# Layer 1 of a convolution-attention hybrid: turning 128x128 squares by DVE and DMA, or by PE

## The chip, the cores and the metric

The kernel runs on one core of a Trainium2 chip. The metric is the device time of one execution in microseconds (us). A core has a matrix engine (TensorE, PE in the profile; its weight loads are listed as PEld), a vector engine (VectorE, DVE), an activation engine (ScalarE, ACT), GpSimd (POOL), and SyncE (SP), which here only issues DMA transfers. Each engine works through a queue of its own, in the order in which the program was laid out for it, and semaphores hold an instruction until what it needs is there. Matrix products go to PSUM, everything else lives in SBUF.

## What is computed

The input x has 4 images of 128 channels and 64x64 pixels, all float32. Two layers follow each other, for each image b:

```python
# layer 0: attention over 4096 pixels, 64 inner channels
q, k, v = wq @ x, wk @ x, wv @ x                 # [64, 4096]
x = x + wo @ (softmax(k.T @ q) @ v.T).T
# layer 1, on tokens t = x.T  [4096, 128]
h = layernorm(t)
t = t + softmax(causal((h @ Wq) @ (h @ Wk).T / sqrt(128))) @ (h @ Wv)
h = layernorm(t)
u = batchnorm(h @ W.T)                           # statistics over all 4 * 4096 tokens
y[n] = sigmoid(u[n] + y[n - 1] @ V.T)            # a scan over the tokens
out = t + y
```

## The kernel before

The whole work sits in `fast_path`. (A second function, `general_path`, runs behind a flag if some number left its safe range; it does not run here.) `xs` keeps all four images in SBUF.

**Blocks and items.** A block is 512 query columns of one image and one layer: 8 blocks of layer 0 and then 8 blocks of layer 1 for each image, 64 in all, 32 of them in layer 1. A block's keys are taken in tiles of 128, two tiles to an item. A layer-0 block has 16 items. A layer-1 block g is causal: it has 2g full items and two partial ones (896 and 384 columns), so the first has 2 items and the last 16. Full layer-1 items take PE about 3.44 us, layer-0 items about 1.72 us.

**One step of the main loop** (L767 to L793) writes down, in this order: the scores of item s (L638: PE products into `s_ps`, then ACT's exponential into `p`, and in layer 1 POOL's causal mask of the diagonal squares); the values of item s - 2 (L699: PE accumulates `acc`); if that item was its block's last, also the copy of `acc` to `agg` (ACT), the sum `den` of the two halves of the denominators (DVE, L733), the row products of a coming block (`r_ps`, L512) and a transposition that was put off; then the sums of item s (L679: DVE adds `p` to `dsum`); and last one task that is due.

**The tasks behind a block.** A generator names each next task with a number of steps. For layer 1 (`finish1`, L583) it is:

- `first`, 1 step after the block's last values: `project` (L517) and `normed` (L536). `project` makes the denominators: `den` holds, for 128 key lanes and 512 queries, sums that must still be added over the 128 lanes, with the result by query on partitions. Four PE transposes put `den` into PSUM (`den_ps`, L521), and one DVE reduce of 128x512 (L523) adds along the free axis. Then a reciprocal (L524), four products with the value weights (`o_ps`, L527) and four DVE updates of the tokens in `xs` (L532). `normed` is the layer norm by tokens, on DVE with one POOL operation: statistics (L541, L542), variance (L544), a power on POOL (L429), three to four tiny DVE operations (L430 to L433), four scalings (L548). Its result is the tile `xh2` (in the profile `xh`).
- `second`, 3 steps later: the tokens before the norm are turned to channels by four PE transposes (`tT_ps`), copied by ACT and stored to DRAM (L596); the normed tokens are turned by four PE transposes as well (`xh2T_ps`, L556) and copied by DVE into `xhT2` (L557).
- `third`, 1 step later: the product with W (`wx_ps`, L602), its batch statistics by DVE (L605) and a copy by ACT into `xs` (L607).

One task runs in a step, the one that has been due longest; where none is due, a piece of the next image's layer-0 keys (`cols0`, `vals0`, `vals0_by_tokens`) is done instead. `finish0` does the same as `first` for layer 0.

**Who sets the order.** The program text gives each engine a sequence, but the framework's scheduler lays the queues out by its own estimate of when an instruction's inputs and buffers are there, so that in the timeline neighbours of the text can be parted, or an instruction can stand ahead of others that precede it in the text. The PSUM tiles of all side work (`den_ps`, `o_ps`, `r_ps`, `tT_ps`, `xh2T_ps`, `wx_ps`, `kr_ps`, ...) share one tag with two banks (`misc`, L443). The pool `work` gives each of its tags two buffers. All transfers in the main loop (`swap<-kr` L475, `xs<-in_xT` L505, `x<-xc` L596) go through SP's queue in order.

**The end.** After the last block, the batch norm's scale is made, and the scan runs in 28 steps of chunks (L825), with the residual and the stores behind it.

Of the kernel before, what the change touches and what calls it, by code (L numbers as in the profile page):

```python
# [9 lines left out]
F32 = mybir.dt.float32  # L10
AF = mybir.ActivationFunctionType
ALU = mybir.AluOpType
AX = mybir.AxisListType
PSUM = bass.MemoryType.PSUM

P = 128
BLK = 512
# [325 lines left out]
def fast_path(  # L343
# [21 lines left out]
    nc = tc.nc  # L365
    B, C, N = x.shape
    M = c_wqT.shape[1]
    assert C == P and M == P // 2 and N % CHUNK == 0
    NT = N // P
    NB = N // BLK  # L370
    TPB = BLK // P
# [2 lines left out]
    WARM, TOL, STEPS = 12, 1e-6, 16  # L374
    NCH = N // STEPS
    CPB = BLK // STEPS

    const = ctx.enter_context(tc.tile_pool(name="const", bufs=1))
    xpool = ctx.enter_context(tc.tile_pool(name="x", bufs=1))
# [32 lines left out]
    ident = const.tile([P, P], F32, name="ident")  # L412
# [6 lines left out]
    nc.gpsimd.memset(mhalf, -0.5)  # L419
    minus = const.tile([P, P], F32, name="minus")  # L420
    nc.vector.tensor_scalar(minus, ident, -1.0, None, ALU.mult)
    good = const.tile([P, 1], F32, name="good")
    g1 = const.tile([P, P], F32, name="g1")
    recs = const.tile([P, 2, B, NT], F32, name="recs")
# [10 lines left out]
    with tc.tile_pool(name="batch", bufs=1) as batch, tc.tile_pool(name="rows", bufs=2) as rowp, tc.tile_pool(  # L435
        name="prob", bufs=4
    ) as prob, tc.tile_pool(name="work", bufs=2) as wk, tc.tile_pool(name="stat", bufs=4) as stat, tc.tile_pool(
        name="ps_s", bufs=2, space=PSUM
    ) as ps_s, tc.tile_pool(name="ps_a", bufs=1, space=PSUM) as ps_a, tc.tile_pool(
        name="ps_m", bufs=2, space=PSUM  # L440
    ) as ps_m:

        def misc(name):  # L443
            return ps_m.tile([P, BLK], F32, tag="m", name=name)
# [72 lines left out]
        def project(layer, b, g, agg, den):  # L517

            dp = misc("den_ps")
            for j in range(TPB):  # L520
                nc.tensor.transpose(dp[:, ts(j, P)], den[:, ts(j, P)], ident)  # L521
            rec = recs[:, layer, b, ts(g, TPB)]
            nc.vector.tensor_reduce(rec, dp.rearrange("p (j k) -> p j k", k=P), AX.X, ALU.add)  # L523
            nc.vector.reciprocal(rec, rec)  # L524
            op = misc("o_ps")
            for j in range(TPB):
                nc.tensor.matmul(  # L527
                    op[:, ts(j, P)], lhsT=agg[:, ts(j, P)], rhs=wv1 if layer else wo2, start=True, stop=True
                )
            for j in range(TPB):  # L530
                t = xs[:, b, ds(g * BLK + j * P, P)]
                nc.vector.scalar_tensor_tensor(  # L532
                    t, in0=op[:, ts(j, P)], scalar=rec[:, j : j + 1], in1=t, op0=ALU.mult, op1=ALU.add
                )

        def normed(b, g, dst):  # L536

            st = stat.tile([P, TPB, nc.vector.BN_STATS_DIM], F32, tag="st", name="ln_st")
            mv = stat.tile([P, TPB, nc.vector.BN_AGGR_DIM], F32, tag="mv", name="ln_mv")
            for j in range(TPB):  # L540
                nc.vector.bn_stats(st[:, j], xs[:, b, ds(g * BLK + j * P, P)])  # L541
                nc.vector.bn_aggr(mv[:, j], st[:, j])  # L542
            var = stat.tile([P, TPB], F32, tag="var", name="ln_var")
            nc.vector.tensor_scalar(var, mv[:, :, 1], LN_EPS, None, ALU.add)  # L544
            y = stat.tile([P, TPB], F32, tag="rstd", name="ln_rstd")
            rsqrt(y, var, stat.tile([P, TPB], F32, tag="z", name="ln_z"))
            for j in range(TPB):
                nc.vector.tensor_scalar(  # L548
                    dst[:, j], xs[:, b, ds(g * BLK + j * P, P)], mv[:, j, 0:1], y[:, j : j + 1], ALU.subtract, ALU.mult
                )  # L550

        def transposed(src, dst, name, engine):

            ps = misc(name)
            for j in range(TPB):
                nc.tensor.transpose(ps[:, ts(j, P)], src[:, j], ident)  # L556
            engine(dst, ps)  # L557

        def in_range():

            r = recs.rearrange("p l b t -> p (l b t)")
            r2 = stat.tile([P, 2 * B * NT], F32, tag="r2", name="r2")
            nc.vector.tensor_scalar(r2, r, LOW, None, ALU.is_ge)
            nc.vector.tensor_scalar(r, r, HIGH, None, ALU.is_le)
            nc.vector.tensor_tensor(r, r, r2, ALU.mult)
            nc.vector.tensor_reduce(good, r, AX.X, ALU.add)

        def finish0(b, g):

            agg, den = bs[b].agg, bs[b].den  # L570

            def norm():
                if g == 0:
                    bs[b].xh = batch.tile([P, NT, P], F32, tag="xh", name="xh")
                    bs[b].xhT = batch.tile([P, N], F32, tag="xhT", name="xhT")
                normed(b, g, bs[b].xh[:, ts(g, TPB)])

            yield 2, lambda: (project(0, b, g, agg, den), norm())
            fill.append(
                lambda: transposed(bs[b].xh[:, ts(g, TPB)], bs[b].xhT[:, ts(g, BLK)], "xhT_ps", nc.scalar.copy)  # L580
            )

        def finish1(b, g):  # L583
            agg, den = bs[b].agg, bs[b].den
            mem = {}

            def first():
                project(1, b, g, agg, den)
                mem["xh"] = wk.tile([P, TPB, P], F32, tag="xh2", name="xh2")
                normed(b, g, mem["xh"])  # L590

            def second():
                t = xs[:, b, ts(g, BLK)].rearrange("p (j c) -> p j c", c=P)
                xc = wk.tile([P, BLK], F32, tag="xc", name="xc")
                transposed(t, xc, "tT_ps", nc.scalar.copy)
                nc.sync.dma_start(out=x2[b, :, ts(g, BLK)], in_=xc)  # L596
                mem["xhT"] = wk.tile([P, BLK], F32, tag="xhT2", name="xhT2")
                transposed(mem["xh"], mem["xhT"], "xh2T_ps", nc.vector.tensor_copy)

            def third():  # L600
                wp = misc("wx_ps")
                nc.tensor.matmul(wp, lhsT=wf, rhs=mem["xhT"], start=True, stop=True)  # L602
                if b == B - 1 and g == NB - 1:
                    in_range()
                nc.vector.bn_stats(stats[:, b * NB + g], wp)  # L605

                nc.scalar.copy(  # L607
                    xs[:, b, ts(g, BLK)].rearrange("p (s c) -> p s c", c=CPB),
                    wp.rearrange("p (c s) -> p s c", s=STEPS),
                )  # L610

            yield 1, first
            yield 3, second
            yield 1, third


        class Item:
# [183 lines left out]
    with tc.tile_pool(name="xr", bufs=1) as xrp, tc.tile_pool(name="y", bufs=2) as yp, tc.tile_pool(  # L801
        name="ps_y", bufs=2, space=PSUM
# [15 lines left out]

        by_step = xs.rearrange("p b (g s c) -> p b s g c", s=STEPS, c=CPB)
        start = xrp.tile([P, B, NCH + 1], F32, name="start")  # L820
        nc.gpsimd.memset(start[:, :, 0:1], 0.0)
        prev = [None] * B
        grid = lambda t: t.rearrange("p (g c) -> p g c", c=CPB)

# [23 lines left out]
        def residual(b):  # L848

            for h in range(2):  # L850
                for g in range(h * NB // 2, (h + 1) * NB // 2):
                    y = yp.tile([P, BLK], F32, tag="yt", name="yt")
                    nc.scalar.copy(  # L853
                        y.rearrange("p (c s) -> p c s", s=STEPS),
                        xs[:, b, ts(g, BLK)].rearrange("p (s c) -> p c s", c=CPB),
                    )
# [10 lines left out]
        for b in range(B):  # L867
# [3 lines left out]
            sq = yp.tile([P, NCH], F32, tag=f"y{b}", name="sq")  # L871
# [69 lines left out]
```

## Time and profile before

| | |
|---|---|
| median of 7 runs | 2188.41 us (2187.5 to 2191.7) |
| the profiled execution | 2190.2 us, its span 2188.4 us |
| PE busy | 2113.9 us, 97% of the span, mean granted clock 0.988 |
| DVE busy | 1440.4 us, 66% |
| ACT busy | 1057.2 us, 48% |
| POOL busy | 104.5 us, 5% |
| 4 x L521 `den_ps`, 64 blocks of both layers | 256 records, 280 ns each by the record |
| 4 x L556 `xh2T_ps`, 32 blocks | 128 records, 285 ns each by the record |
| L523 reduce of `den_ps` (DVE) | 64 records, 684 ns each |
| L557 copy of `xh2T_ps` (DVE) | 32 records, 691 ns each |
| L602 `wx_ps` | 64 records (two for each product) |
| L596 `x<-xc`, issue on SP / to landing | 0.32 us / 2.0 us |
| L475 `swap<-kr`, issue on SP / to landing | 0.47 us / 2.2 us |
| L505 `xs<-in_xT`, issue on SP / to landing | 0.46 us / 3.1 us |

In span order there is a start of some 34 us (loads and the first keys), then for each image about 238 us of layer 0 and 275 us of layer 1, and from 2075 us on the tail with the scan. PE runs matrix instructions pipelined, so the lengths of its records overlap: what a group really occupies is read from the starts of the groups before and behind it, or from the chain of waits. An f32 product is two records, an f32 transpose one. "Idle before" is the time in which an engine stood still before an instruction, with the instruction that ended the wait.

### The profile page before, as it was taken

What the parts mean: (1) busy time and instruction counts of PE and PEld (TensorE: products, weight loads), DVE (VectorE), ACT (ScalarE), POOL (GpSimd) and SP (SyncE); (2) the same over time, 40 slices, a digit from 0 to 9 for tenths busy, and PEclk for the clock granted to TensorE, in tenths of its full rate; (3) what the DMA queues carried; (4) which work ended last, traced back from release to release, by engine and by line L of the source; (5) the groups of instructions that cost most, each with busy time, mean ns of one, the idle gap of its engine ahead of it and who ended that gap; (6) DMA issues with size and microseconds to landing.
All of it is one profiled execution on the core that took longest, in us unless ns stands there. A gap on an engine that the chain in (4) does not pass through costs nothing.

```text
span 2188.4 us, 30521 instructions
## 1 busy us (share of the span) xinstructions
PE 2113.9 (97%) x12204; PEld 940.7 (43%) x12204; DVE 1440.4 (66%) x2703; ACT 1057.2 (48%) x1162; POOL 104.5 (5%) x207
## 2 busy tenths in 40 slices
PE   6999999999999999999999999999999999999973
PEld 2333354444333345444333335444433334544452
DVE  2888865444788875544588886445488887544486
ACT  3666633333566643333466653333356664333278
POOL 0000010000000010000000001000000001000000
PEclk9999999999999999999999999999999999999986
DMA  6000011000000001000000001100000000000033
GB/s 222 1 1 1 1 30 49 5 5 5 6 1 1 1 15 44 20 10 5 6 1 1 1 1 39 39 5 6 5 6 1 1 1 6 10 10 5 6 159 155
DMA packets 30134, 48.74 MB, mean 22 GB/s; under 512 B 3104, under 2 KB 20256, under 8 KB 28448
## 3 DMA queue, kind: packets, MB, share of 16 engines
q1 hardware_dynamic: 28096, 46.15, 6.1%
q8 instruction: 98, 1.61, 0.3%
q10 hardware_dynamic: 1888, 0.56, 0.1%
q14 instruction: 52, 0.43, 0.1%
HBM read 25.72 MB, written 16.78 MB: 19 GB/s over the span
## 4 chain that ended last, share of the span: by engine, by line
PE 91%; ACT 4%; DVE 2%; DMA 1%; POOL 0%; issue 0%; SPq 0%; ACTq 0%; DVEq 0%
PE s_ps L658 21%; PE acc L717 21%; PE s_ps L649 20%; PE acc L709 19%; PE o_ps L527 2%; ACT yt L853 1%; PE den_ps L521 1%; PE wx_ps L602 1%; ACT xs L841 1%; PE r_ps L512 1%; PE kr_ps L469 1%; ACT y L841 1%; PE xhT_ps L556 1%; DVE dsum L689 1%; PE xh2T_ps L556 1%; PE v_ps L481 1%
## 5 line engine op out<-in xcount | busy, mean ns | idle before, releaser
L689 DVE TENSOR_TENSOR dsum<-dsum,p 128x1024 f32<-128x1024 f32 x676 | 828.0, 1225 | 466.0 <-ACT p L665 336.7
L663 ACT ACTIVATE p<-s_ps,nshift 128x1024 f32<-128x1024 f32 x512 | 571.4, 1116 | 357.5 <-PE s_ps L649 338.0
L665 ACT ACTIVATE p<-s_ps 128x1024 f32<-128x1024 f32 (+2 forms) x288 | 274.2, 952 | 564.0 <-PE s_ps L658 462.5
L709 PE MATMUL acc<-p,v 64*64 64x512 f32 x4096 | 532.5, 590 | 1.7 <-ACT half L728 1.7
L649 PE MATMUL s_ps<-swap,kr 64*64 64x512 f32 x2048 | 530.0, 595 | 1.9 <-DMA swap<-kr 1.9
L649 PE MATMUL s_ps<-kr 64*64 64x512 f32 x2048 | 530.0, 595 | 0.0
L658 PE MATMUL s_ps<-rows,xhT 128*128 128x512 f32 (+3 forms) x1152 | 504.0, 559 | 0.0
L717 PE MATMUL acc<-p,xh 128*128 128x512 f32 (+3 forms) x1152 | 501.6, 558 | 0.0
L717 PEld LDWEIGHTS acc<-p,xh 128*128 128x128 f32 x1152 | 216.1, 191 | 240.8 <-issue 231.4
L658 PEld LDWEIGHTS s_ps<-rows,xhT 128*128 128x128 f32 x1152 | 211.4, 190 | 226.7 <-issue 189.4
L709 PEld LDWEIGHTS acc<-p,v 64*64 64x64 f32 x4096 | 155.6, 133 | 284.5 <-issue 265.5
L649 PEld LDWEIGHTS s_ps<-swap,kr 64*64 64x64 f32 x2048 | 137.6, 133 | 133.1 <-issue 123.9
L649 PEld LDWEIGHTS s_ps<-kr 64*64 64x64 f32 x2048 | 137.6, 133 | 128.2 <-issue 123.6
L429 POOL TENSOR_TENSOR ln_rstd<-ln_var,mhalf 128x4 f32<-128x4 f32 x64 | 66.1, 1033 | 1221.3 <-DVE ln_var L544 1221.3
L697 DVE TENSOR_TENSOR dsum<-dsum,p 128x256 f32<-128x256 f32 (+1 forms) x120 | 55.9, 499 | 72.4 <-POOL p L669 72.4
L687 DVE COPY dsum<-p 128x1024 f32<-128x1024 f32 x60 | 41.4, 690 | 69.7 <-ACT p L665 57.6
L532 DVE SCALAR_TENSOR_TENSOR xs<-o_ps,recs,xs 128x128 f32<-128x128 f32 x256 | 73.0, 344 | 8.9 <-PE o_ps L527 2.8
L548 DVE TENSOR_SCALAR xh<-xs,ln_mv,ln_rstd 128x128 f32<-128x128 f32 x256 | 71.3, 342 | 2.2
L669 POOL TENSOR_SCALAR_AFFINE_SELECT p<-p 128x128 f32<-128x128 f32 x128 | 34.4, 292 | 681.8 <-ACT p L665 681.8
L541 DVE BATCH_NORM_STATS2 ln_st<-xs 128x6 f32<-128x128 f32 x256 | 63.5, 270 | 0.0
L607 ACT COPY xs<-wx_ps 128x512 f32<-128x512 f32 x32 | 18.7, 584 | 69.5 <-DVE stats L605 69.5
L840 DVE SCALAR_TENSOR_TENSOR z<-xs,scale,y_ps 128x256 f32<-128x256 f32 x108 | 48.5, 480 | 4.9 <-DMA xr<-x 3.4
(101 smaller groups left out, 1106.6 us busy)
## 6 DMA issues: line engine op xcount, KB each, us to landing
xs<-in_x SPq DMA_DIRECT2D x16, 512.0 KB, 8.4
xs<-in_xT SPq DMA_DIRECT2D x32, 256.0 KB, 3.1
x<-xc SPq DMA_DIRECT2D x32, 256.0 KB, 2.0
xr<-x SPq DMA_DIRECT2D x4, 2048.0 KB, 12.0
out_x<-xr SPq DMA_DIRECT2D x8, 1024.0 KB, 3.9
swap<-kr SPq DMA_DIRECT2D x32, 128.0 KB, 2.2
wo<-in_c_woT ACTq DMA_DIRECT2D x2, 32.0 KB, 4.3
wqT<-in_a_wqT ACTq DMA_DIRECT2D x1, 64.0 KB, 5.5
```

The lines of the kernel that those rows point to most:

```text
L429: nc.gpsimd.tensor_tensor(y, var, mhalf[:, : y.shape[-1]], ALU.pow)
L532: nc.vector.scalar_tensor_tensor(t, in0=op[:, ts(j, P)], scalar=rec[:, j : j + 1], in1=t, op0=ALU.mult, op1=ALU.add)
L541: nc.vector.bn_stats(st[:, j], xs[:, b, ds(g * BLK + j * P, P)])
L548: nc.vector.tensor_scalar(dst[:, j], xs[:, b, ds(g * BLK + j * P, P)], mv[:, j, 0:1], y[:, j : j + 1], ALU.subtract, ALU.mult)
L649: nc.tensor.matmul(ps[c * M : c * M + M, off : off + n], lhsT=bs[it.b].kr[part, h, ds(t % (NT // 2) * P + c * M, M)], rhs=rows[h], start=True,
L658: nc.tensor.matmul(ps[:, off : off + n], lhsT=lhsT, rhs=rhs, start=True, stop=True)
L663: nc.scalar.activation(it.p[:, :off], ps[:, :off], AF.Exp, bias=nshift)
L665: nc.scalar.activation(it.p[:, :off], ps[:, :off], AF.Exp, scale=float(P) ** -0.5)
L689: nc.vector.tensor_tensor(flat, flat, it.p, ALU.add)
L697: nc.vector.tensor_tensor(den[:, h, q0:], den[:, h, q0:], it.p[:, o : o + n], ALU.add)
L709: nc.tensor.matmul(bt.acc[h * M : h * M + M, r], lhsT=bt.v[part, t], rhs=it.p[part, o : o + n], start=it.first, stop=it.last,)
L717: nc.tensor.matmul(bt.acc[:, 0, q0:], lhsT=bt.xh[:, t], rhs=it.p[:, o : o + n], start=it.first and h == 0, stop=it.last and h == 1,)
```

## The change

It touches layer 1 alone, and of it two places; layer 0 keeps its PE transposes.

- **Denominators** (`project`, all 32 layer-1 blocks). In place of four PE transposes and a DVE reduce, DVE turns `den` in squares of 32x32 (`sq`), and one DVE reduce adds each square's rows: `part`, 128 partitions by 16 columns. One PE product with a constant matrix `fold` (the identity folded to add the four 32-partition groups and repeat the sum on each) gives 16 columns, of which each partition needs four: DVE multiplies by the mask `quarter` (`own`) and reduces to the four columns of `rec`.
- **Normed tokens** (`finish1`, 31 of the 32 blocks; the last keeps the old way). In place of four PE transposes and a DVE copy, DVE turns the tokens in 32x32 squares into `sqT`, and 16 transfers on SP's queue, each of 32 partitions by four runs of 128 bytes, place the squares in `xhT2`. For these blocks `third` comes 4 steps after `second` instead of 1.
- Two constants, `fold` and `quarter`, are built by eight DVE operations at the start. A scratch tile of the range test moves into the tag `den`.

```diff
--- before.py
+++ after.py
@@ -374,6 +374,8 @@
     WARM, TOL, STEPS = 12, 1e-6, 16
     NCH = N // STEPS
     CPB = BLK // STEPS
+    S = nc.vector.STREAM_SQUARE_SIZE
+    Q = P // S
 
     const = ctx.enter_context(tc.tile_pool(name="const", bufs=1))
     xpool = ctx.enter_context(tc.tile_pool(name="x", bufs=1))
@@ -419,6 +421,17 @@
     nc.gpsimd.memset(mhalf, -0.5)
     minus = const.tile([P, P], F32, name="minus")
     nc.vector.tensor_scalar(minus, ident, -1.0, None, ALU.mult)
+    fold = const.tile([P, P], F32, name="fold")
+    nc.vector.tensor_reduce(
+        fold[:, :S], ident.rearrange("p (q r) -> p r q", r=S), AX.X, ALU.add
+    )
+    for q in range(1, Q):
+        nc.vector.tensor_copy(fold[:, ts(q, S)], fold[:, :S])
+    quarter = const.tile([P, TPB, Q], F32, name="quarter")
+    for j in range(TPB):
+        nc.vector.tensor_reduce(quarter[:, j], ident.rearrange("p (q r) -> p q r", r=S), AX.X, ALU.add)
     good = const.tile([P, 1], F32, name="good")
     g1 = const.tile([P, P], F32, name="g1")
     recs = const.tile([P, 2, B, NT], F32, name="recs")
@@ -517,10 +530,24 @@
         def project(layer, b, g, agg, den):
 
             dp = misc("den_ps")
-            for j in range(TPB):
-                nc.tensor.transpose(dp[:, ts(j, P)], den[:, ts(j, P)], ident)
             rec = recs[:, layer, b, ts(g, TPB)]
-            nc.vector.tensor_reduce(rec, dp.rearrange("p (j k) -> p j k", k=P), AX.X, ALU.add)
+            if layer:
+                sq = wk.tile([P, TPB * Q, S], F32, tag="sq", name="sq")
+                nc.vector.transpose(out=sq.rearrange("p a b -> p (a b)"), in_=den)
+                part = stat.tile([P, TPB * Q], F32, tag="part", name="part")
+                nc.vector.tensor_reduce(part, sq, AX.X, ALU.add)
+                nc.tensor.matmul(dp[:, : TPB * Q], lhsT=fold, rhs=part, start=True, stop=True)
+                own = stat.tile([P, TPB, Q], F32, tag="own", name="own")
+                nc.vector.tensor_tensor(
+                    own, dp[:, : TPB * Q].rearrange("p (j q) -> p j q", q=Q), quarter, ALU.mult
+                )
+                nc.vector.tensor_reduce(rec, own, AX.X, ALU.add)
+            else:
+                for j in range(TPB):
+                    nc.tensor.transpose(dp[:, ts(j, P)], den[:, ts(j, P)], ident)
+                nc.vector.tensor_reduce(rec, dp.rearrange("p (j k) -> p j k", k=P), AX.X, ALU.add)
             nc.vector.reciprocal(rec, rec)
             op = misc("o_ps")
             for j in range(TPB):
@@ -559,7 +586,7 @@
         def in_range():
 
             r = recs.rearrange("p l b t -> p (l b t)")
-            r2 = stat.tile([P, 2 * B * NT], F32, tag="r2", name="r2")
+            r2 = wk.tile([P, BLK], F32, tag="den", name="r2")[:, : 2 * B * NT]
             nc.vector.tensor_scalar(r2, r, LOW, None, ALU.is_ge)
             nc.vector.tensor_scalar(r, r, HIGH, None, ALU.is_le)
             nc.vector.tensor_tensor(r, r, r2, ALU.mult)
@@ -583,6 +610,7 @@
         def finish1(b, g):
             agg, den = bs[b].agg, bs[b].den
             mem = {}
+            final = b == B - 1 and g == NB - 1
 
             def first():
                 project(1, b, g, agg, den)
@@ -595,7 +623,18 @@
                 transposed(t, xc, "tT_ps", nc.scalar.copy)
                 nc.sync.dma_start(out=x2[b, :, ts(g, BLK)], in_=xc)
                 mem["xhT"] = wk.tile([P, BLK], F32, tag="xhT2", name="xhT2")
-                transposed(mem["xh"], mem["xhT"], "xh2T_ps", nc.vector.tensor_copy)
+                if final:
+                    transposed(mem["xh"], mem["xhT"], "xh2T_ps", nc.vector.tensor_copy)
+                    return
+                sq = wk.tile([P, Q, TPB, S], F32, tag="sqT", name="sqT")
+                nc.vector.transpose(
+                    out=sq.rearrange("p c j t -> p j c t"), in_=mem["xh"].rearrange("p j (c r) -> p j c r", r=S)
+                )
+                to = mem["xhT"].rearrange("p (j q t) -> p j q t", q=Q, t=S)
+                for c in range(Q):
+                    for q in range(Q):
+                        nc.sync.dma_start(out=to[ts(c, S), :, q], in_=sq[ts(q, S), c])
 
             def third():
                 wp = misc("wx_ps")
@@ -611,7 +650,7 @@
 
             yield 1, first
             yield 3, second
-            yield 1, third
+            yield 1 if final else 4, third
 
 
         class Item:
```

## The prediction

> **What bounds the kernel now.** I read the shares and the chain first, then the busy time by stretches, then the timeline at the places the change touches. The page says which engine carries the end:
>
> ```profile
> PE 2113.9 (97%) x12204; PEld 940.7 (43%) x12204; DVE 1440.4 (66%) x2703; ACT 1057.2 (48%) x1162; POOL 104.5 (5%) x207
> PE 91%; ACT 4%; DVE 2%; DMA 1%; POOL 0%; issue 0%; SPq 0%; ACTq 0%; DVEq 0%
> ```
>
> 91% of the chain that ended last is TensorE (PE) work. By stretches (columns: stretch, its length, busy us and instructions of PE, weight load, DVE, ACT, POOL, then PE clock and DMA), the dense first blocks of layer 1, a passage from layer 1 to the next batch's layer 0, a layer-0 part and a layer-1 part:
>
> ```profile
> 270.00:300.00 30.00, 30.00 (x128) 15.08 (x121) 20.33 (x62) 10.86 (x15) 4.56 (x10) 1.00 0.11 27
> 545.00:560.00 15.00, 13.82 (x112) 5.68 (x104) 10.92 (x29) 7.71 (x8) 1.01 (x1) 1.00 0.05 18
> 560.00:790.00 230.00, 228.92 (x2061) 86.48 (x2062) 189.54 (x301) 145.54 (x137) 7.84 (x9) 1.00 0.01 1
> 820.00:1060.00 240.00, 240.00 (x700) 116.45 (x699) 119.95 (x242) 78.08 (x93) 12.48 (x30) 1.00 0.06 18
> ```
>
> In layer 1 PE is busy without a gap at clock 1.00, and VectorE (DVE) is idle half of it (120 of 240 us), a third of it in the dense first blocks (20.3 of 30). PE has holes only in the passages (13.8 of 15). So PE time taken out of layer 1 should come off the span, unless PE is made to wait.
>
> **What goes and what comes on PE.** The chain shows what four pipelined transposes really occupy (start, length):
>
> ```profile
> 365.27 1.72 PE acc L717 x4
> 366.99 0.44 PE den_ps L521 x4
> 367.43 0.89 PE o_ps L527 x8
> 368.32 1.72 PE s_ps L658 x4
> ```
>
> Not the 280 ns of one record, which overlap, but 0.44 us for four; eight 128-column records take 0.89, so 0.111 each.
>
> - Normed tokens: 31 of 32 blocks lose four transposes, in the timeline 346.62 to 347.06: 31 x 0.44 = 13.6 us.
> - Denominators: 32 blocks lose 0.44 and gain one 16-column f32 product, two records as every f32 product here. No row has that width. If cost went with columns, 2 x 0.111 x 16/128 = 0.03; if the weight load sets it, 2 x 0.111 = 0.22; if its two 0.19 us loads were not hidden as well, 0.60. I take 0.22, the row with the same 128x128 weights: 32 x 0.22 = 7.0 us saved (13.1 to -5.1).
>
> Together 20.6 us less PE work.
>
> **What DVE gets.** Denominators: a transpose of 128x512, a reduce as large as the present one (0.68, L523), and two ops of 128x16, near the 0.16 to 0.18 us of the small rows (L430 to L433, L524). No DVE transpose is in the trace. A 128x512 copy or add takes 0.69; a 128x1024 copy from SBUF also takes 0.69 (L687), so 0.35 is the low end and 1.4, twice the 0.69 row, the high end. I take 0.69: +1.03 us a block, 33 us in all (22 to 56). Tokens: the transpose takes the place of the 0.69 us copy L557: nothing (-0.35 to +0.7 a block). The cover is DVE's idle half: blocks come every 10 to 60 us. Without the cover, 33 us would be the price. The constants at the start (eight ops of at most 128x128, 0.2 to 0.3 us each) lie in the 13.3 us that DVE waits for L448: nothing. At the very end den is ready at 2077.42, PE free at 2078.74; transpose and reduce end at 2078.8, and the updates L532 wait for o_ps until 2080.78 anyway: nothing. Dropping the token PSUM tile only frees a bank early: nothing.
>
> [...]
>
> **The new wait in the denominators.** PE's product now needs DVE's transpose and reduce; PE takes its queue in order, so o_ps and the next scores stand behind it. In program order they follow the step's dsum. But the queues are not laid in program order:
>
> ```profile
> 352.93 0.69 DVE L697 TENSOR_TENSOR dsum<-dsum,p 128x256 f32<-128x256 f32 x2 [0.90 <-POOL p L669]
> ...
> 353.66 0.69 DVE L733 TENSOR_TENSOR den<-dsum 128x512 f32<-128x512 f32 x1
> ...
> 357.75 0.69 DVE L687 COPY dsum<-p 128x1024 f32<-128x1024 f32 x1 [3.40 <-ACT p L665]
> ```
>
> den is made 13 us before PE reaches its transposes (366.99) and before the next block's first sum, which precedes it in the program; DVE then idles 3.4 us. Transpose and reduce (1.4 us) fit there. I take no wait. DVE's "own" waits for PE 0.3 us; behind it stands only work that needs the reciprocal.
>
> **The new wait for the tokens.** Per block SP issues 16 transfers of 16 KB; the product L602 needs them all. Issue rows: x<-xc 0.32, xs<-in_xT 0.46, swap<-kr 0.47 us; landing 2.0 to 2.2 for x and swap. So 16 x 0.39 + 2.1 = 8.4 us after the transpose (7.1 to 9.7). L602 moves from one step to four steps behind "second". In a layer-1 block: tokens normed at 374.23; the fourth step after 380.11 ends near 394.3. Transpose as late as the present copy (381.87): landed by 391.6. Covered, with 2.7 us left. Behind them on SP stand only the x2 store, swap and tokens of a later stage, needed tens of us on; POOL gets nothing.
>
> The three passages are otherwise, since four layer-0 steps are short (1.72 us each):
>
> ```profile
> 556.33 1.12 DVE L548 TENSOR_SCALAR xh<-xs,ln_mv,ln_rstd 128x128 f32<-128x128 f32 x4
> 556.73 1.10 PE L556 MATMUL xh2T_ps<-ident,xh 128*128 128x128 f32 x4 [0.89 <-DVE xh L548]
> 557.36 2.55 DVE L689 TENSOR_TENSOR dsum<-dsum,p 128x1024 f32<-128x1024 f32 x2
> ...
> 560.66 1.10 PE L602 MATMUL wx_ps<-xhT,wf 128*128 128x512 f32 x2 [0.95 <-DVE xhT L557]
> ```
>
> Here PE now waits 0.89 + 0.95 = 1.84 us; that goes. New: tokens ready at 557.45; the transpose ends at 558.1, or at 560.6 behind the two sums, mean 559.4; + 8.4 = 567.8. L602's place: tT_ps at 555.18 + 0.44, four steps of 1.72: 562.5. PE waits 5.3, less 1.84: +3.5 us, three times +10.4. With the quick ends 0.9 each (+2.6), with the slow ones 6.0 (+18). The fourth such block has no new wait: the last is left on PE.
>
> [...]
>
> **Sum.** -20.6 + 10.4 = -10.2 us. The profiled execution took 2190.2 us (span 2188.4), 1.8 above the median 2188.41, inside the runs' 2187.5 to 2191.7; on it the sum makes 2180, and from the median, which the result is compared with, 2178.
>
> **Rivals.**
> 1. *No wait in the passages*: L602 is laid behind further steps until its transfers are in. For it: den_ps and o_ps are parted by scores at 285.9 while a buffer is held, so the layout does avoid waits. Against: it was early by about 1 us in both passage waits above, and a serial queue of 16 issues is new. -20.6 - 5.5 = -26: 2162; with the 0.03 us product 2156. Chance 0.23.
> 2. *The denominators stop PE* (slower): if transpose and reduce stay behind the step's sum (366.45 + 1.23), the product can start at 369.06, PE is there at 366.99: 2.07 us, 32 times 66 us. -10.2 + 66: 2244. It decides from 0.32 us a block. For it: program order, and the in-order queue. Against: den's place. Chance 0.12.
> 3. *Slow transfers*: at 0.93 us an issue (twice swap) and the transpose midway (378.4), the transfers land at 395.5, 1.2 us late in some 28 blocks: 33 us; the passages cost 26 more: 2237. With the early transpose (374.9) layer 1 is covered up to 1.08 us. For it: 128 runs of 128 bytes each, unlike any row. Against: 512 runs issue in 0.46. Chance 0.13, half of it below 2205.
> 4. *It doesn't shorten anything*: PE is lighter, but DVE, with 9.7 us idle in the dense 30, is what scores wait for there. The same time within 0.2%: 2188. Chance 0.10.
>
> **Chances.** My forecast 0.42, between 2170 and 2186 by its ends. 0.2% (4.4 us) is about what a measurement of this kernel can tell from no change. Faster: 0.36 of the forecast's 0.42, rival 1, 0.02 of rival 4: 0.61. Same: 0.06 of the forecast, 0.06 of rival 4, 0.02 of rival 3: 0.14. Slower: 0.12 + 0.11 + 0.02: 0.25. The range 2160 to 2205 leaves out rival 2, half of rival 3 and the cheapest product, near 0.2.
>
> **What would show it.** Right: PE in layer 1 still busy without holes, fewer PE instructions, den_ps product near 0.22 us in the chain, DVE transposes near 0.69 soon behind den, PE waiting some 5 us for DMA at three L602 only. Wrong: idle PE ahead of the den_ps product with DVE as releaser (rival 2), ahead of L602 in every block (rival 3), or ahead of scores with DVE sums as releaser (rival 4); or an SP issue well off 0.39 us.

## The result, and the profile after

| | before | changed |
|---|---|---|
| median of the runs | 2188.41 us (35 runs) | 2194.98 us (15 runs) |
| ratio, 95% interval | | 1.0028 [1.0022, 1.0035] |
| span of the profiled execution | 2188.4 us | 2194.0 us |

The change makes the kernel 6.6 us slower; the forecast was 10 us faster. Line numbers behind the changed places are higher now: `den_ps` by the 16-column product is L541, o_ps L554, wx_ps L641, the transfers of the squares L637.

The page after, shares and chain by engine:

```profile
PE 2098.7 (96%) x12016; PEld 920.7 (42%) x12016; DVE 1470.8 (67%) x2807; ACT 1058.4 (48%) x1162; POOL 104.7 (5%) x207
PE 91%; ACT 3%; SPq 2%; DMA 2%; DVE 1%; issue 0%; POOL 0%; ACTq 0%; DVEq 0%
```

PE has 15 us less to do, and yet the end comes later. New in the chain is SP's queue (SPq) with 2% of the span, and DMA has 2% in place of 1%. The stretches say where. These are the four of before, and a fifth over the next passage (columns as before):

```profile
270.00:300.00 30.00, 29.66 (x118) 15.31 (x117) 21.48 (x70) 11.22 (x15) 4.14 (x10) 1.00 0.10 27
545.00:560.00 15.00, 11.04 (x100) 3.69 (x92) 12.15 (x26) 7.64 (x8) 1.01 (x1) 0.98 0.11 26
560.00:790.00 230.00, 225.84 (x2008) 84.69 (x2012) 183.94 (x296) 141.67 (x133) 7.74 (x8) 0.98 0.01 2
820.00:1060.00 240.00, 240.00 (x693) 114.60 (x696) 127.74 (x262) 80.29 (x96) 12.49 (x30) 1.00 0.11 26
1060.00:1085.00 25.00, 16.15 (x139) 6.30 (x136) 15.56 (x34) 9.51 (x9) 1.01 (x1) 0.86 0.10 22
```

Layer 1 is as forecast: PE 240.00 of 240.00 us, DVE with 8 us more. The loss is in the passages, where 16.15 of 25 us are busy, and there the granted clock falls to 0.86; in the kernel before this stretch was:

```profile
1060.00:1085.00 25.00, 23.16 (x188) 9.01 (x190) 17.60 (x36) 12.69 (x13) 1.01 (x1) 1.00 0.03 12
```

One row of PE's list of waits is new (engine, what waited, for what; total, times, longest):

```profile
PE wx_ps L641 <- DMA xhT<-sqT: 26.6, 4, 8.8
```

Four waits, not one in every block. Three are the passages; the fourth is in the first layer-1 block of the last image:

```profile
1870.49 1.10 PE L641 MATMUL wx_ps<-xhT,wf 128*128 128x512 f32 x2 [2.02 <-DMA xhT<-sqT]
```

The timeline of the first passage shows how one comes about:

```profile
550.50 0.71 DVE L631 STREAM_TRANSPOSE sqT<-xh 128x512 f32<-128x512 f32 x1
...
551.28 7.02 SPq L637 DMA_DIRECT2D xhT<-sqT  x11
...
558.40 0.53 SPq L624 DMA_DIRECT2D x<-xc  x1
558.98 3.17 SPq L637 DMA_DIRECT2D xhT<-sqT  x5
563.73 2.05 PE L641 MATMUL wx_ps<-xhT,wf 128*128 128x512 f32 x2 [7.69 <-DMA xhT<-sqT]
565.71 1.12 PE L688 MATMUL s_ps<-swap,kr 64*64 64x512 f32 x2
```

DVE is in time and quick (0.71). SP then issues eleven transfers in 7.02 us, the x2 store that stands in the same queue, and five more: the last leaves at 562.15, and PE starts at 563.73 after 7.69 us of waiting. The products behind the hole last 1.12 us where the same product elsewhere takes 0.60.

The chain through the denominators, to be held against the four rows of before:

```profile
361.21 1.72 PE acc L756 x4
362.93 0.13 PE den_ps L541 x2
363.06 0.99 PE o_ps L554 x8
364.05 1.72 PE s_ps L697 x4
```

No wait ahead of the product: 0.13 + 0.99 us in place of 0.44 + 0.89.

### The profile page after: what moved, and what is told of

Same layout as the page of the kernel before. It is cut to its first block, busy times and chain, and to the rows that moved or that the text cites. A ratio compares the mean times of both kernels' runs of the same rounds, so it can differ in the third digit from the quotient of the medians.

```text
span 2194.0 us, 30942 instructions
## 1 busy us (share of the span) xinstructions
PE 2098.7 (96%) x12016; PEld 920.7 (42%) x12016; DVE 1470.8 (67%) x2807; ACT 1058.4 (48%) x1162; POOL 104.7 (5%) x207
## 4 chain that ended last, share of the span: by engine, by line
PE 91%; ACT 3%; SPq 2%; DMA 2%; DVE 1%; issue 0%; POOL 0%; ACTq 0%; DVEq 0%
PE s_ps L697 20%; PE s_ps L688 20%; PE acc L756 20%; PE acc L748 20%; PE o_ps L554 3%; SPq L637 2%; PE wx_ps L641 1%; ACT yt L892 1%; ACT xs L880 1%; PE r_ps L525 1%; PE y_ps L877 1%; PE kr_ps L482 1%; PE den_ps L549 1%; PE xhT_ps L583 1%; PE tT_ps L583 1%; PE v_ps L494 1%
## 5 line engine op out<-in xcount | busy, mean ns | idle before, releaser
L641 PE MATMUL wx_ps<-xhT,wf 128*128 128x512 f32 x64 | 36.9, 660 | 27.5 <-DMA xhT<-sqT 26.6
```

## The experiments

The theory after the result (H): the change does what it should in layer 1, and loses it in three passages from layer 1 to the next image's layer 0, where PE waits for 16 transfers issued one after another on one queue, and then runs slowly for a while, at a granted clock of 0.50 for 10.24 us each. The rivals: the new path from DVE over PE to DVE in the denominators costs it (D); or the transfers and SP's queue slow everything (Q).

### 1. The product later in the passages alone

```diff
-            yield 1 if final else 4, third
+            yield 1 if final else (10 if g == NB - 1 else 4), third
```

> The product wx_ps of an image's last block comes 10 steps after its second task instead of 4; nothing else is changed. Theory H (three holes of 7.7 to 8.9 us at the passages, where PE waits for 16 transfers issued 0.64 us apart, and about 2.3 us of slow products behind each hole): ten layer-0 steps are 17 us, so the three holes and their slow products go, 24.6 + 7 us: 2195 - 32 = 2163 us. Rival D (the new DVE-PE-DVE path of the denominators costs it): no change, 2195. Rival Q (SP's queue and the transfers slow everything down): within 5 us of 2195.

Measured: 2166.82 us against 2189.55 of before on the same chip, ratio 0.9896 [0.9881, 0.9911]. 28 us come back by one number. The stretch of the first passage:

```profile
545.00:575.00 30.00, 29.18 (x258) 9.81 (x254) 24.48 (x38) 18.94 (x20) 1.01 (x1) 1.00 0.09 19
```

against 22.31 busy at clock 0.83 for the same stretch of the changed kernel. All transfers are still there. D and Q fall as causes of the loss; H stands, some 4 us short of its number. The profile shows most of these: the wait at the fourth place is still there, and now the products behind it are slow, which takes them 1.7 us longer; and ahead of the next values after each passage PE waits 0.82 us for ACT's `half`, where it waited 0.43.

### 2. The last block of each image back on PE

```diff
-                if final:
+                if g == NB - 1:
                     transposed(mem["xh"], mem["xhT"], "xh2T_ps", nc.vector.tensor_copy)
...
-            yield 1 if final else 4, third
+            yield 1 if g == NB - 1 else 4, third
```

> The last block of each image keeps PE transposes and the early third task for its tokens, the other 28 blocks keep transfers. Theory H: the three holes go, 3 x 0.44 us of transposes and 3 x 1.84 us of the old waits come back: 2195 - 32 + 7 = 2170 us, 6 to 7 above the run with the late product. Rival D: 2195. Rival Q: 2195 less a tenth of what the transfers cost, some 2193.

Measured: 2172.78 us, ratio 0.9925 [0.9911, 0.9938], 6.0 us above the late product, where 6 to 7 were expected: with no transfers in the passages the loss is gone too, and the old waits and transposes are back.

### 3. and 4. Each part alone

For the denominators alone every block's tokens are turned by PE, with one step to the third task; for the tokens alone layer 1 takes the old path of `project`.

```diff
# denominators alone
-                if final:
+                if True:
...
-            yield 1 if final else 4, third
+            yield 1, third
# tokens alone
-            if layer:
+            if False:
```

> Only the denominators go by DVE squares and the 16-column product; tokens are turned by PE in all blocks, third task 1 step later, as before. Theory H: 32 x 0.22 us saved, 2188.4 - 7 = 2181 us. Rival D: above 2195, since the tokens' saving of 13.6 us is gone too. Rival Q: 2181.

> Only the tokens go by DVE squares and transfers (31 blocks, 4 steps); denominators by PE transposes as before. Theory H: the holes stay, the 7 us of the denominators are lost: 2195 + 7 = 2202 us. Rival D: 2188 - 13.6 = 2175. Rival Q: 2202.

Measured: denominators alone 2186.38 us, ratio 0.9989 [0.9980, 0.9998]; tokens alone 2196.97 us, 1.0038 [1.0025, 1.0052]. D wanted the first above 2195 and the second at 2175; both go against it. H and Q ask for the same numbers here, and the signs are theirs, but both runs miss these numbers by 5 us: the denominators save 3.2 us, not 7 (2.0 by the step from the tokens alone to the whole change). Taken from the starts of successive PE groups in the traces (before against denominators alone), `den_ps` takes 9.3 us less in all, the o_ps groups behind it 2.5 more, the `acc` groups of layer 1 ahead of it 2.2 more and the `tT_ps` groups 1.3 more. So the product saved more than I thought, and its neighbours took most of that back. Why `acc` and `tT_ps` lengthen wasn't tested.

### 5. and 6. How long the hole is, and what the clock does

```diff
-            yield 1 if final else 4, third
+            yield 1 if final else (6 if g == NB - 1 else 4), third     # run 6: 8
```

> As the changed kernel, but the last block of an image has its product wx_ps 6 steps after its second task instead of 4. [...] If the slow products belonged to the transfers in flight and not to the length of the hole, they would stay as they are also with a short hole. Rival (the scheduler, not the step, places the product): 2195.

> The same with 8 steps: 6.9 us off each hole, which leaves 0.8 to 2 us. If the clock's drop depends on the hole's length, the slow products (some 2.3 us behind each hole) go as well: 2195 - 20.6 - 7 = 2167.5 us, and products behind the remaining wait last 0.6 us as elsewhere. If the slow products belong to the transfers, 2174.

Measured: 6 steps 2186.47 us, ratio 0.9989 [0.9979, 0.9998]; 8 steps 2170.34 us, 0.9916 [0.9899, 0.9932]. With 4, 6, 8 and 10 steps: 2195.0, 2186.5, 2170.3, 2166.8. From 4 to 6 the fall is 8.5 us, not quite three times two steps (3 x 3.44 = 10.3); from 6 to 8 it is 16.1, far more, because here the slow products go too. 6 steps, PE in the first passage:

```profile
565.08 2.04 PE L641 MATMUL wx_ps<-xhT,wf 128*128 128x512 f32 x2 [5.30 <-DMA xhT<-sqT]
567.05 1.12 PE L688 MATMUL s_ps<-swap,kr 64*64 64x512 f32 x2
```

8 steps, the same place:

```profile
565.40 1.10 PE L641 MATMUL wx_ps<-xhT,wf 128*128 128x512 f32 x2 [1.32 <-DMA xhT<-sqT]
566.42 0.65 PE L688 MATMUL s_ps<-swap,kr 64*64 64x512 f32 x2
```

After 5.30 us of waiting the same product takes 2.04 us, after 1.32 us 1.10. All transfers are made in both, so the slow products come with the longer hole and not with the transfers. Mean granted clock over 545 to 575: 0.83 with 4 steps, 0.89 with 6, 1.00 with 8.

### 7. Sixteen transfers with long runs

The squares are laid out so that each transfer is 32 partitions by one run of 512 bytes; the product reads its columns through a rearranged view.

```diff
-                to = mem["xhT"].rearrange("p (j q t) -> p j q t", q=Q, t=S)
+                to = mem["xhT"].rearrange("p (q j t) -> p q j t", q=Q, t=S)
...
-                        nc.sync.dma_start(out=to[ts(c, S), :, q], in_=sq[ts(q, S), c])
+                        nc.sync.dma_start(out=to[ts(c, S), q], in_=sq[ts(q, S), c])
...
-                nc.tensor.matmul(wp, lhsT=wf, rhs=mem["xhT"], start=True, stop=True)
+                rhs = mem["xhT"] if final else mem["xhT"].rearrange("p (q j t) -> p j q t", q=Q, t=S)
+                nc.tensor.matmul(wp, lhsT=wf, rhs=rhs, start=True, stop=True)
```

> As the changed kernel (4 steps), but the turned tokens are laid out so that each of the 16 transfers is 32 partitions by one run of 512 bytes instead of four of 128; the product reads its columns through a rearranged view. Theory R (the issue time of 0.60 us comes from the 128 short runs): issue 0.35 to 0.45, 16 x 0.2 = 3 us off each hole: 2195 - 10 = 2185 us. Rival F (a fixed price of a transfer of this kind): issue 0.6, 2195. A rearranged view that slows the product's columns would add up to 31 x 0.9 us: above 2195.

Measured: 2194.03 us, ratio 1.0024 [1.0014, 1.0034]. Theory R falls. The issue rows (min/median/max in ns), here with a quarter of the runs:

```profile
L637 SPq DMA_DIRECT2D xhT<-sqT x496: 507/588/1444, 304.3 to 2055.1; - x166
```

and in the changed kernel:

```profile
L637 SPq DMA_DIRECT2D xhT<-sqT x496: 585/599/1631, 300.8 to 2054.3; - x166
```

588 ns with 32 runs against 599 with 128: of what an issue takes here, the runs set next to nothing. Other sizes were not tried.

### 8. Half of the transfers from POOL

```diff
-                        nc.sync.dma_start(out=to[ts(c, S), :, q], in_=sq[ts(q, S), c])
+                        (nc.gpsimd if q % 2 else nc.sync).dma_start(out=to[ts(c, S), :, q], in_=sq[ts(q, S), c])
```

> As the changed kernel (4 steps), but half of the 16 transfers is issued by POOL. Theory H (the holes are 16 serial issues of 0.64 us on one queue): eight issues less on SP, 5 us off each hole, 2.6 to 3.8 us left, if POOL issues in at most 0.64 us each and its own work (the power of the norm, the mask) is not held up: 2195 - 15 to - 22, so 2173 to 2180 us. If the transfers' landing set the holes, no change: 2195. If POOL issues at over 1.2 us each: 2195 or above.

Measured: 2173.48 us, ratio 0.9926 [0.9909, 0.9943], in the range of H. POOL issues in 0.55 us. The first passage:

```profile
553.31 6.17 SPq L637 DMA_DIRECT2D xhT<-sqT  x8
553.54 4.38 POOL L637 DMA_DIRECT2D xhT<-sqT  x8 [4.00 <-DVE sqT L631]
559.59 0.53 SPq L624 DMA_DIRECT2D x<-xc  x1
561.20 1.10 PE L641 MATMUL wx_ps<-xhT,wf 128*128 128x512 f32 x2 [3.15 <-DMA xhT<-sqT]
```

Nothing but the queue was changed, and the wait falls from 7.69 to 3.15 although one of SP's issues lasted 1.67 us here: the serial issue set most of it. Landing is as long as before (median 1.9 us for SP's transfers and 1.7 for POOL's, against 1.8).

### 9. Both cures

Run 1 and run 8 together (10 steps in the passages, two queues).

> Both cures: 10 steps for the last block of an image, and half of the transfers issued by POOL. Theory H: no hole is left at any wx_ps, also not the fourth one of 2 us in the last image's first layer-1 block: 2167 - 2 = 2165 us. If POOL's issuing (0.55 us each) holds up the norm's power or the mask, 2167 or above.

Measured: 2164.52 us, ratio 0.9892 [0.9877, 0.9907], where 2165 was expected. PE's waits for transfers at wx_ps are gone from the list, the fourth one too. Against run 1 it is 2.3 us less; the two intervals overlap, so the step from one to the other is not shown by the times.

### 10. The same for the tokens before the norm

This is on top of run 9.

```diff
-                transposed(t, xc, "tT_ps", nc.scalar.copy)
-                nc.sync.dma_start(out=x2[b, :, ts(g, BLK)], in_=xc)
+                if final:
+                    transposed(t, xc, "tT_ps", nc.scalar.copy)
+                    nc.sync.dma_start(out=x2[b, :, ts(g, BLK)], in_=xc)
...
+                xq = xc.rearrange("p (c j t) -> p c j t", c=Q, t=S)
+                nc.vector.transpose(
+                    out=xq.rearrange("p c j t -> p j c t"), in_=t.rearrange("p j (c r) -> p j c r", r=S)
+                )
+                rows = x2[b, :, ts(g, BLK)].rearrange("(c r) (j q t) -> q c r j t", r=S, q=Q, t=S)
+                for q in range(Q):
+                    for c in range(Q):
+                        (nc.gpsimd if c % 2 else nc.sync).dma_start(out=rows[q, c], in_=xq[ts(q, S), c])
...
-            yield 1 if final else (10 if g == NB - 1 else 4), third
+            yield 1 if final else (12 if g == NB - 1 else 6), third
```

> In addition the tokens before the norm are turned by DVE and stored to DRAM by 16 more transfers of 16 KB, in place of four PE transposes and an ACT copy, in 31 blocks; the product wx_ps comes 6 steps after, 12 in the passages. If PE time taken out of layer 1 comes off the span wherever PE isn't made to wait: 31 x 0.44 = 13.6 us less, 2165 - 14 = 2151 us. If DVE (31 x 0.71 us more) or 32 transfers a block are now late: 2165 or above, with PE holes behind DVE sums or transfers.

Measured: 2148.74 us, ratio 0.9820 [0.9807, 0.9834]: 15.8 us below run 9, where 13.6 were expected (the ACT copies of 31 blocks go too, and the third task comes two steps later). The stretch of layer 1:

```profile
820.00:1060.00 240.00, 240.00 (x772) 112.00 (x774) 134.28 (x273) 81.81 (x93) 68.85 (x134) 1.00 0.13 24
```

PE still has no gap, with DVE at 134 us of 240 and 32 transfers a block (POOL's 69 us are mostly its issues). Runs 1, 2, 6, 8 and 9 take 0.7 to 1.1% less than the kernel before, and this one 1.8%.

## Why the prediction was wrong

- **What bounds, and that PE time comes off**: right. Layer 1 ran without a gap in the stretch shown, and run 10 took 15.8 us off the end with 13.6 us of PE transposes, by the prediction's price.
- **Tokens, 13.6 us of PE time**: right, and somewhat too small. From run 3 to run 2, 28 blocks' tokens move to transfers and 13.6 us go, 0.49 a block and not 0.44. By the starts of successive groups the `xh2T_ps` groups take 17.5 us before and 2.1 in the changed kernel, 15.4 less.
- **Denominators, 7.0 us**: mis-sized. Alone they gave 3.2 (0.4 to 4.4 by the interval). The product itself costs 0.13 to 0.17 us, less than the 0.22 taken; the groups around it took back 6 of the 9.3 us.
- **DVE**: the transpose takes 0.71 us (0.69 taken). No stretch shows it as the bound.
- **The new wait in the denominators** (rival 2): right that there is none. In the changed kernel the squares follow `den` directly, as its old place suggested:

```profile
350.07 0.69 DVE L772 TENSOR_TENSOR den<-dsum 128x512 f32<-128x512 f32 x1
...
350.80 0.71 DVE L538 STREAM_TRANSPOSE sq<-den 128x512 f32<-128x512 f32 x1
...
351.54 0.69 DVE L540 TENSOR_REDUCE part<-sq 128x16 f32<-128x512 f32 x1
```

- **The new wait for the tokens**: this is the step that failed, by its size. The mechanism and the three places were right. The prediction took 16 x 0.39 us + 2.1 = 8.4 us from transpose to landing, a wait of 5.3 us and a price of +3.5 us a passage. Measured: 0.60 us for each issue and 0.04 between two, the x2 store (0.53) among them, 12.5 us from the transpose's end at 551.21 to the product's start; waits of 7.69, 8.85 and 8.02 us. Of these 12.5 us 10.3 lie between the first issue and the last, and the last transfer landed 1.8 us after its issue began, less than the 2.1 taken. The rows taken for the issue (0.32 to 0.47) were of other shapes, and the range's bound, 0.47, was too low. The prediction named the doubt in rival 3 and in its last line, but it tried 0.93 only with late transfers in layer 1 as well; 0.64 lies between, late in the passages and in time in all but one of the other blocks.
- **A term was missing**: PE's clock, granted at 0.50 for 10.24 us at each passage. Behind each hole wx_ps, one item's scores and one group of values last 5.5, 4.9 and 5.0 us, where the same run of products takes 2.8 in the run with 8 steps: 7 us in three passages. With the three measured waits alone the prediction's sum would have been -20.6 + 3 x (8.2 - 1.84) = -1.5 us; it takes this term and the denominators' 3.8 us to make a loss of it.
- **The fourth wait**: 2.02 us in the dense first block of the last image's layer 1. The prediction worked out a later block, covered with 2.7 us to spare, and not the first ones.

The sum with measured terms: -15.4 - 3.2 + 3 x (8.2 - 1.84) + 7 + 2.0 = +9.5, and the 0.86 us that PE waited before at the fourth place (ahead of `xh2T_ps` at 1848.55) come off: +8.6, against +6.6 measured (4.8 to 7.7 by the interval). 2 us are not accounted for. The two profiled executions, 5.6 us apart, hold a difference that isn't the change's: the first image's first values block ends 2.6 us earlier in the changed kernel's. Over 30 to 40 us, PE's granted clock is 0.83 in the profile of before and 1.00 in that of the changed kernel; it is 0.66 in run 7 and 0.83 in runs 8 and 9, whose edits leave the changed kernel's start alone, and there that block is late too. So the early block isn't owed to the new start. How often the other executions lost this time isn't known.

## What to carry to other kernels

A change that takes work off the bounding engine is paid where its new latency meets the shortest steps: work out the slack at every kind of place, the passages between stages first, and not only in the steady state. Sixteen small transfers on one queue cost here sixteen times the issue (0.60 us each), and a quarter of the runs left it at 0.59; with no row of the same shape, take a bound well above the known rows (here 0.32 to 0.47). And a wait of the matrix engine can be charged twice, once as the hole and once as the slow products behind it: here, from 30 us on, holes of 3.15 us and more always were, holes of up to 1.77 us in the main loop never, and between the two it went either way.

## What was not expected of the hardware

PE's slow products. In the changed kernel PE's granted clock is 0.50 for 10.24 us at each of the three passages, from 559.38, 1078.20 and 1597.03 on, the end of the hole included; wx_ps then takes 2.04 us and the scores 1.12. The old kernel had it too, at its very end: 3.69 us of waiting ahead of the last `xh2T_ps`, then 2.04 for wx_ps. The length of the hole alone doesn't decide. Holes of 1.15 to 2.02 us left the clock at 1.00 in the changed kernel and in runs 2, 5 and 6, but 2.08 and 2.56 us in run 8 were followed by 0.50 for 3.41 us, and so was run 1's hole at the fourth place, shorter than the 2.02 us of the changed kernel at the same place:

```profile
1840.29 1.87 PE L641 MATMUL wx_ps<-xhT,wf 128*128 128x512 f32 x2 [1.93 <-DMA xhT<-sqT]
```

What tells them apart can be worked out from the traces. The half clock lasts 3.41 us in the kernel before, from 34.31 on, and three times as long, 10.24, at the changed kernel's passages; its starts there lie 518.82 and 518.83 us apart, 152 times 3.413 each. Cut into intervals of this length, counted from where the half clock starts, run 1's hole fills 1.93 us of one interval, and the next one has half the clock; of the changed kernel's 2.02 us, 1.63 lie in one interval and the rest in the next, and the clock stays (columns as before; the first two rows are run 1, the others the changed kernel):

```profile
1837.06:1840.47 3.41, 1.48 (x5) 0.44 (x4) 3.34 (x7) 0.10 (x1) 0.99 (x2) 1.00 0.16 25
1840.47:1843.88 3.41, 3.41 (x5) 1.33 (x5) 1.46 (x3) 0.58 (x1) 0.00 (x0) 0.50 0.16 24
1866.69:1870.10 3.41, 1.78 (x5) 0.47 (x3) 3.31 (x8) 0.49 (x1) 0.98 (x2) 1.00 0.16 24
1870.10:1873.51 3.41, 3.02 (x7) 1.44 (x8) 1.93 (x3) 0.69 (x2) 0.00 (x0) 1.00 0.16 24
```

From 30 to 2050 us of the two kernels' traces, the full-clock intervals with 3.34, 2.98 and 2.22 us of idle PE (the changed kernel's passages) and with 2.38 (the old kernel, from 30.90 on) are each followed by half the clock, and none with 1.63 or less. Past 2050 us the changed kernel's clock also fell after an interval with 1.82 us (from 2085.13 on). No run moved a hole within its interval to test this, so it is no more than what these traces show.

A transfer of 16 KB between 32-partition squares takes SP's queue 0.60 us to issue, more than one of 256 KB with 512 runs (0.46 in the kernel before), with 32 runs (0.59) as with 128; from POOL it takes 0.55. Landing took 1.8 us, the median.
